# The gate's and the value's last 42 columns of a gated feed-forward as one joint block of weights

## Chip, cores and metric

The kernel runs on one core of one Trainium2 chip. The metric is the device time of one execution in microseconds (us); the time before is the median of three runs.

## What is computed

The reference runs two layers of a perceiver on x of shape 32 x 64 x 256 with a context of 32 x 1601 x 256. Each layer is a cross-attention, a self-attention or recurrent block and a feed-forward. The change concerns the gated feed-forward at the end of the recurrent block of layer 1, cut to what matters:

```
FF_INNER = int(D * 4 * 2 / 3)              # 682 with D = 256
n = _rmsnorm(x, ff_gamma)
ff = jax.nn.silu(n @ w_gate) * (n @ w_value) @ w_ff_out
x = ff * RES_SCALE + x
```

682 is 5 x 128 + 42: five full blocks of 128 columns, and a rest of 42.

## The kernel before

The 2048 rows of x are worked in 16 tiles of 128 rows. The bulk of the time is a software pipeline over the cross-attention of layer 1: 13 steps for each tile, 208 in all. Each step g issues, in this order, the column scores of g (L773, L779, then the exponential on ACT, L785), the values of g + 4 (tile vps; copied by DVE to vau, L715), the row scores of g + 5 (L731, tile r; their maxima on DVE, L738, tile mx), the weighted sum of g (L803) and the keys of g + 6 (tile kps; copied by ACT to kt, L698). The column scores and the row scores share two pairs of PSUM banks (tag sc), so the column scores of a step wait until DVE has taken the maxima of the row scores issued before.

All other layers' work is put between these parts by generators. Each `yield` is a place where a generator may stop; `yield ACT` asks to go on in the slot between values and row scores (place 0), a bare `yield` in the slot after the keys (place 1). The order on PE, DVE, ACT and POOL is the order in which the program is written and run through (a manual schedule); the DMA issues on SP are put in by the framework. The generator `tail` of one tile runs `recurrent` and then `bit_ffn`; the gated feed-forward is the last part of `recurrent`. Beside it, in the same slots, run the generators of later tiles: `query` (tp_d, copied by ACT to xT_d, then the product q) and `layer0` (tp_c, su, sv, k, q, v, tpp, o, gps).

Every small product of PE goes to one of three PSUM banks, which all these generators and vps and kps share (`mm_tile`, tag mm, three buffers). Which bank a product gets, and whose end it then waits for, is decided by the framework from the order in which earlier users give their banks back.

The feed-forward takes the normalised rows, transposed, as nT (two chunks of 128). w_fg and w_fv hold the gate's and the value's weights as six blocks of 128 columns, the last padded with zeros from column 682. The work is done in two halves of three blocks each. Per half, mm2 (L233) multiplies three blocks of the gate into one bank, then three of the value into another; an fp32 matmul is issued as two instructions, so a half has 24. Then `silu_mul` follows: tanh of half the gate on ACT (L237, tile fth), half the gate on DVE (L238, tile fm), times the value (L239), and after a yield (tanh + 1) times that (L241). The last product ffo (L946) multiplies the six blocks of fm with w_fo, whose rows past 682 are zero. In 14 of the tiles both halves fall into the pipeline; the last two tiles are worked after it, in the last 75 us, where nothing else is left to run beside them. There the seven DVE steps of the last tile's convolution (cT, L863 and L866) stand in DVE's queue behind the products of the tile before.

The weights of this part are loaded by SP in `late_weights`, between 24 and 51 us, among the loads of parts of the context (part, L95), each of which waits for ACT to have summed up the one before (L245). The first feed-forward begins at 365 us.

Of the kernel before, what the change touches and what calls it, by code (L numbers as in the profile page):

```python
# [9 lines left out]
F32 = mybir.dt.float32  # L10
BF16 = mybir.dt.bfloat16
AF = mybir.ActivationFunctionType
ALU = mybir.AluOpType
AX = mybir.AxisListType

P = 128
# [8 lines left out]
FF = 682  # L25
NF = 6
# [18 lines left out]
def perceiver_kernel(ctx: ExitStack, tc: tile.TileContext, a: dict, out: bass.AP):  # L45
    nc = tc.nc
    PSUM = bass.MemoryType.PSUM

    const = ctx.enter_context(tc.tile_pool(name="const", bufs=1))
# [19 lines left out]
    def mm_tile(shape, name, dtype=F32):  # L69
        return ps_mm.tile(shape, dtype, tag="mm", name=name)  # L70
# [115 lines left out]
    def moments(x, name):  # L186

        st = small.tile([P, 6], F32, tag="bnst", name=f"st_{name}")
        nc.vector.bn_stats(st, x)
        mv = small.tile([P, 2], F32, tag="bnmv", name=f"mv_{name}", bufs=4)  # L190
        nc.vector.bn_aggr(mv, st)
        rstd = small.tile([P, 1], F32, tag="rstd", name=f"rstd_{name}", bufs=4)
        nc.gpsimd.tensor_scalar(rstd, mv[:, 1:2], 1e-5, None, ALU.add)
        nc.gpsimd.tensor_tensor(rstd, rstd, mhalf, ALU.pow)
        return x, mv, rstd
# [34 lines left out]
    def mm2(o, lhsT, rhs):  # L230

        for c in range(2):
            nc.tensor.matmul(o, lhsT=lhsT(c), rhs=rhs(c), start=(c == 0), stop=(c == 1))  # L233

    def silu_mul(m, u, v, th):

        nc.scalar.activation(th, u, AF.Tanh, scale=0.5)  # L237
        nc.vector.tensor_scalar(m, u, 0.5, None, ALU.mult)  # L238
        nc.vector.tensor_tensor(m, m, v, ALU.mult)  # L239
        yield  # L240
        nc.vector.scalar_tensor_tensor(m, th, 1.0, m, ALU.add, ALU.mult)  # L241
# [603 lines left out]
    def recurrent(ti, x):  # L845
        def tile_(shape, tag, name):
            return work_tile(shape, tag, f"{name}_{ti}")

        m = moments(x, f"e{ti}")
# [8 lines left out]
        for c in range(2):  # L858
            nc.scalar.activation(ypad[:, c, :, 3:], t[:, c, :].rearrange("p (b s) -> p b s", b=2), AF.Copy,
                                 scale=gains[:, c, 0:1])  # L860
# [17 lines left out]
        nT = tile_([P, 2, P], "xTb", "nT")  # L878
# [14 lines left out]
        for part in range(2):  # L893
            for c in range(2):
                for h in range(2):
                    r = slice(64 * h, 64 * h + 64)
# [34 lines left out]
        nT = tile_([P, 2, P], "xTb", "nT2")  # L931
# [1 line left out]
            nc.scalar.activation(nT[:, c, :], t[:, c, :], AF.Copy, scale=gains[:, c, 2:3])  # L933
        yield ACT
        m = tile_([P, NF, P], "w4k", "fm")
        for f0 in range(0, NF, 3):
            uv = [mm_tile([P, 3, P], f"ff_{ti}_{f0}_{j}") for j in range(2)]
            for o, w in zip(uv, (w_fg, w_fv)):
                for f in range(3):
                    mm2(o[:, f, :], lambda c: w[:, c, (f0 + f) * P:(f0 + f + 1) * P], lambda c: nT[:, c, :])  # L940
            th = tile_([P, 3, P], "g2k", f"fth{f0}")
            yield from silu_mul(m[:, f0:f0 + 3, :], uv[0], uv[1], th)
            yield ACT if f0 == 0 else None
        o = mm_tile([P, D], f"ffo_{ti}")
        for f in range(NF):
# [54 lines left out]
    def tail(ti, x):  # L1000
        x = yield from recurrent(ti, x)
        yield from bit_ffn(ti, x)
# [36 lines left out]
    w_hg = const.tile([P, 2, 2 * DI], F32, name="w_hg")  # L1039
    w_go = const.tile([P, 4, 64], F32, name="w_go")  # L1040
    nc.gpsimd.memset(w_go[DI:], 0.0)
    w_fg = const.tile([P, 2, NF * P], F32, name="w_fg")
    w_fv = const.tile([P, 2, NF * P], F32, name="w_fv")
    for w in (w_fg, w_fv):
        nc.gpsimd.memset(w[:, :, FF:], 0.0)
    w_fo = const.tile([P, NF, D], F32, name="w_fo")
    nc.gpsimd.memset(w_fo[:, NF - 1, :], 0.0)

    def late_weights():
        for j in range(4):  # L1050
            nc.sync.dma_start(w_o2[32 * j:32 * j + 16],
                              a["L1_xattn_WoT"].rearrange("(g j d) o -> j d g o", j=4, d=16)[j])
            nc.sync.dma_start(bv2[32 * j:32 * j + 16], a["bv2"][j])
        nc.sync.dma_start(w_pw, a["L1_attn_pw_wT"].rearrange("(c p) o -> p c o", p=P))
        nc.sync.dma_start(w_hg, a["L1_attn_w_hg"].rearrange("(c h) d e -> (h d) c e", c=2))
        nc.sync.dma_start(w_go[:DI], a["L1_attn_w_out"].rearrange("h e o -> e h o"))
        for w, name in ((w_fg, "L1_attn_w_gate"), (w_fv, "L1_attn_w_value")):
            nc.sync.dma_start(w[:, :, :FF], a[name].rearrange("(c p) f -> p c f", p=P))
        last = (NF - 1) * P
        nc.sync.dma_start(w_fo[:, 0:NF - 1, :], a["L1_attn_w_ff_out"][0:last, :].rearrange("(f p) o -> p f o", p=P))  # L1060
        nc.sync.dma_start(w_fo[0:FF - last, NF - 1, :], a["L1_attn_w_ff_out"][last:FF, :])

# [159 lines left out]
    with tc.manual_schedule(engines={ET.PE, ET.DVE, ET.Activation, ET.Pool}):  # L1222
# [43 lines left out]
        for g in range(NU * NT):  # L1266
            pos, p = divmod(g, NU)
# [80 lines left out]
```

## Time and profile before

| | before |
|---|---|
| median of 3 runs | 2189.57 us (2186.16 to 2190.60) |
| profiled execution | 2185.15 us, span 2183.4 us |
| granted TensorE clock, mean | 0.977 |
| PE busy | 2065.7 us, 95% |
| DVE busy | 1342.4 us, 61% |
| ACT busy | 907.6 us, 42% |
| POOL busy | 325.6 us, 15% |
| matmuls ff<-nT,w_fg and ff<-nT,w_fv | 384 each, 51.6 and 49.1 us busy |
| DVE L238, L239, L241 on fm | 32 each, 17.8, 17.7 and 17.6 us busy |
| ACT L237 on fth | 32, 15.7 us busy |

A matmul's busy time overlaps with that of its neighbours, since matmuls are pipelined: the record of one 128x128 matmul is 275 ns long, while the next begins after 112 ns. What a matmul costs is therefore read from the starts. An entry "idle before <-X" names what the engine waited for. A span's time is from the first to the last instruction; the execution's own time is 1.75 us longer.

### The profile page before, as it was taken

The page shows a single profiled execution, that of the slowest core. Times are in us where ns is not written, and L with a number is a line of the kernel's source. Part 1 is how long each engine was busy: PE and PEld are TensorE (multiplying, and loading weights), DVE is VectorE, ACT ScalarE, POOL GpSimd, SP SyncE. Part 2 cuts the span into 40 slices and gives each one's busy share as a digit, 9 for nine tenths or more (in the row PEclk, how much of TensorE's full clock was granted, in tenths as well). Part 3 has the DMA queues.
Part 4 walks back from the last instruction along what each step waited for, and adds up shares of the span by engine and source line. Part 5 has one row for each costly group of instructions (what it writes and reads, how often), then busy time and mean ns, then how long its engine had stood idle before and what let it go on. Part 6 is the DMA issues. An engine that isn't in the chain of part 4 may idle for free.

```text
span 2183.4 us, 69814 instructions
## 1 busy us (share of the span) xinstructions
PE 2065.7 (95%) x31887; PEld 1510.1 (69%) x31903; DVE 1342.4 (61%) x2710; ACT 907.6 (42%) x1400; POOL 325.6 (15%) x541
## 2 busy tenths in 40 slices
PE   5799999999999999999999999999999999999984
PEld 3567677767677777777777676777777676677763
DVE  4556756666656766666666656566676665556554
ACT  3334444443535344454544435453433434334342
POOL 2111111111111111111111111111110111000011
PEclk8799999999999999999999999999999999999996
DMA  7233221211112121111211111110101101010000
GB/s 265 80 111 113 79 74 55 78 53 35 67 62 70 62 67 35 64 67 62 69 65 35 56 61 65 65 52 32 35 24 44 53 32 35 8 38 35 2 5 5
DMA packets 46176, 126.42 MB, mean 58 GB/s; under 512 B 12558, under 2 KB 28344, under 8 KB 45880
## 3 DMA queue, kind: packets, MB, share of 16 engines
q1 hardware_dynamic: 45320, 121.13, 16.2%
q8 instruction: 250, 4.10, 0.8%
q10 hardware_dynamic: 560, 0.81, 0.1%
q14 instruction: 46, 0.38, 0.1%
HBM read 119.83 MB, written 2.10 MB: 56 GB/s over the span
## 4 chain that ended last, share of the span: by engine, by line
PE 83%; DVE 11%; ACT 3%; issue 1%; DMA 1%; POOL 1%; SPq 0%; POOLq 0%; ACTq 0%; DVEq 0%
PE vps L233 16%; PE kps L233 15%; PE r L731 10%; PE o L803 9%; PE s L779 8%; PE ff L233 4%; DVE mx L738 3%; PE s L773 3%; PE ffo L946 2%; DVE vau L715 2%; PE q L233 1%; PE wo L838 1%; ACT pt L785 1%; PE hg L897 1%; PE v L319 1%
## 5 line engine op out<-in xcount | busy, mean ns | idle before, releaser
L738 DVE TENSOR_REDUCE mx<-r 128x2 f32<-128x1024 f32 x384 | 452.2, 1220 | 118.5 <-PE r L731 118.1
L785 ACT ACTIVATE pt<-s 128x1024 f32<-128x1024 f32 (+1 forms) x416 | 403.0, 1020 | 293.5 <-PE s L779 293.3
L698 ACT ACTIVATE kt<-kps,chv 128x512 f32<-128x512 f32 x192 | 131.9, 687 | 640.2 <-PE kps L233 640.2
L233 PE MATMUL vps<-w_L_xattn_WvT,ctxT 128*128 128x128 f32 x3072 | 395.1, 282 | 0.0
L233 PE MATMUL kps<-ctxT,w_L_xattn_WkT 128*128 128x512 f32 x768 | 383.2, 622 | 11.9 <-DMA ctxT<-ctxT 11.9
L233 PEld LDWEIGHTS vps<-w_L_xattn_WvT,ctxT 128*128 128x128 f32 x3072 | 359.0, 192 | 23.7 <-issue 2.8
L715 DVE COPY vau<-vps 128x512 f32<-128x512 f32 (+1 forms) x208 | 143.3, 689 | 373.0 <-PE vps L233 372.9
L803 PEld LDWEIGHTS o<-pt,vau 128*32 128x32 f32 (+1 forms) x13312 | 197.4, 110 | 150.9 <-issue 144.1
L803 PE MATMUL o<-pt,vau 128*32 128x64 f32 (+1 forms) x13312 | 232.0, 222 | 4.2 <-ACT pt L785 4.2
L731 PE MATMUL r<-kt,qbd 32*128 32x512 f32 x1536 | 228.1, 652 | 2.5 <-DVE mx L738 1.5
L233 PEld LDWEIGHTS kps<-ctxT,w_L_xattn_WkT 128*128 128x128 f32 x768 | 131.6, 191 | 123.7 <-issue 106.8
L779 PEld LDWEIGHTS s<-qbd,kt 32*128 32x128 f32 x6144 | 206.3, 187 | 3.1
L779 PE MATMUL s<-qbd,kt 32*128 32x128 f32 x6144 | 206.6, 271 | 0.0
L245 ACT ACTIVATE part<-part 128x1601 f32<-128x1601 f32 x60 | 92.6, 1543 | 15.8 <-DMA part<-ctxT 15.6
L731 PEld LDWEIGHTS r<-kt,qbd 32*128 32x128 f32 x1536 | 63.3, 185 | 40.9 <-issue 18.7
L773 PEld LDWEIGHTS <-onesb 3*128 3x128 bf16 x768 | 20.8, 91 | 91.3 <-issue 89.7
L773 PE MATMUL s<-neg,onesb 3*128 3x512 bf16 x768 | 79.0, 385 | 5.1 <-DVE mx L738 2.9
L821 DVE RECIPROCAL rs<-sums 128x128 f32<-128x128 f32 x64 | 60.7, 948 | 1.7 <-PE sums L818 1.7
L311 POOL TENSOR_TENSOR kbd<-kT,mask 128x512 f32<-128x512 f32 x32 | 32.9, 1049 | 138.0 <-ACT kT L304 138.0
L233 PE MATMUL ff<-nT,w_fg 128*128 128x128 f32 x384 | 51.6, 287 | 1.0 <-ACT nT L933 1.0
L233 PE MATMUL ff<-nT,w_fv 128*128 128x128 f32 x384 | 49.1, 278 | 0.0
L233 PEld LDWEIGHTS ff<-nT,w_fg 128*128 128x128 f32 x384 | 47.7, 200 | 1.8 <-ACT nT L933 1.6
(334 smaller groups left out, 2543.5 us busy)
## 6 DMA issues: line engine op xcount, KB each, us to landing
ctxT<-ctxT SPq DMA_DIRECT2D x32, 1601.0 KB, 7.1
part<-ctxT SPq DMA_DIRECT2D x60, 800.5 KB, 4.4
rest<-ctxT SPq DMA_DIRECT2D x32, 65.0 KB, 2.0
x<-x SPq DMA_DIRECT2D x16, 128.0 KB, 2.1
out<-x SPq DMA_DIRECT2D x16, 128.0 KB, 1.7
w<-w SPq DMA_DIRECT2D x16, 128.0 KB, 2.2
sum_L_ffn_w1T<-L_ffn_w1T SPq DMA_DIRECT2D x4, 256.0 KB, 6.6
raw_L_ffn_w1T<-L_ffn_w1T SPq DMA_DIRECT2D x4, 256.0 KB, 2.6
```

The lines of the kernel that those rows point to most:

```text
L233: nc.tensor.matmul(o, lhsT=lhsT(c), rhs=rhs(c), start=(c == 0), stop=(c == 1))
L245: nc.scalar.activation(junk, src, AF.Copy, accum_out=csum[:, c, b:b + 1])
L698: nc.scalar.activation(kt, o, AF.Identity, bias=chv[:, hf.oc, BK2:BK2 + 1])
L715: nc.vector.tensor_copy(v[:kr, :, 0:VW - 16].rearrange("p k (h d) -> p k h d", d=17)[:, :, :, 0:16], o[:kr].rearrange("p k (h d) -> p k h ...
L731: nc.tensor.matmul(o, lhsT=qbd[r, q % 2, q // 2].rearrange("p h q -> p (h q)"), rhs=w.kt[r, q, :] if h is None else halves[h].kt[k][r, :], ...
L738: nc.vector.tensor_reduce(w.mx[:, 2 * m:2 * m + 2, h % 4, k], ps[m], AX.X, ALU.max)
L773: nc.tensor.matmul(o, lhsT=onesb[r, :], rhs=halves[h].neg[r, :].unsqueeze(1).to_broadcast([3, 4, P]), start=True, stop=False)
L779: nc.tensor.matmul(ps[i // 2][:kr, i % 2, j * P:(j + 1) * P], lhsT=w.kt[r, j, :] if h is None else halves[h].kt[k][r, j * P:(j + 1) * P], ...
L785: nc.scalar.activation(pt[:kr].rearrange("p i k c -> p i (k c)"), ps[m][:kr], AF.Exp)
L803: nc.tensor.matmul(w.o[32 * c:32 * c + 32, q, m, :], lhsT=v[:kr, j, 17 * hd:17 * hd + 32], rhs=pts[m][:kr, c // 2, j, c % 2 * S:c % 2 * S ...
L821: nc.vector.reciprocal(rs, t)
L946: nc.tensor.matmul(o, lhsT=m[:, f, :], rhs=w_fo[:, f, :], start=(f == 0), stop=(f == NF - 1))
```

## The change

The second half keeps two full blocks each of gate and value. The two rests of 42 columns go into one block of weights, w_fl, the gate's at columns 0 to 41 and the value's at 64 to 105, zeros elsewhere. It is multiplied once, as the last of the half, into the third part of the gate's bank, so that the gate's rest comes out on partitions 0 to 41 and the value's rest on partitions 64 to 105 of the same columns. Tanh and halving run over all three parts as before. The multiplication by the value is split: two blocks from the value's bank, and the rest by a 64-row product that reads partitions 64 to 127 of the gate's bank and writes partitions 0 to 63 of fm. Rows 64 to 127 of the last part of fm then hold numbers that meet only zero rows of w_fo. The code of `silu_mul` is written out in place (now L946 to L953); its steps are the same in the first half.

```diff
-        for f0 in range(0, NF, 3):
+        for f0, n in ((0, 3), (3, 2)):
             uv = [mm_tile([P, 3, P], f"ff_{ti}_{f0}_{j}") for j in range(2)]
             for o, w in zip(uv, (w_fg, w_fv)):
-                for f in range(3):
+                for f in range(n):
                     mm2(o[:, f, :], lambda c: w[:, c, (f0 + f) * P:(f0 + f + 1) * P], lambda c: nT[:, c, :])
             th = tile_([P, 3, P], "g2k", f"fth{f0}")
-            yield from silu_mul(m[:, f0:f0 + 3, :], uv[0], uv[1], th)
+            if f0:
+
+                mm2(uv[0][:, 2, :], lambda c: w_fl[:, c, :], lambda c: nT[:, c, :])
+            u = uv[0][:, 0:3]
+            nc.scalar.activation(th, u, AF.Tanh, scale=0.5)
+            mf = m[:, f0:f0 + 3, :]
+            nc.vector.tensor_scalar(mf, u, 0.5, None, ALU.mult)
+            nc.vector.tensor_tensor(mf[:, 0:n], mf[:, 0:n], uv[1][:, 0:n], ALU.mult)
+            if f0:
+                nc.vector.tensor_tensor(mf[0:64, 2], mf[0:64, 2], uv[0][64:128, 2], ALU.mult)
+            yield
+            nc.vector.scalar_tensor_tensor(mf, th, 1.0, mf, ALU.add, ALU.mult)
             yield ACT if f0 == 0 else None
...
-    w_fg = const.tile([P, 2, NF * P], F32, name="w_fg")
-    w_fv = const.tile([P, 2, NF * P], F32, name="w_fv")
-    for w in (w_fg, w_fv):
-        nc.gpsimd.memset(w[:, :, FF:], 0.0)
+    w_fg = const.tile([P, 2, (NF - 1) * P], F32, name="w_fg")
+    w_fv = const.tile([P, 2, (NF - 1) * P], F32, name="w_fv")
+    w_fl = const.tile([P, 2, P], F32, name="w_fl")
+    nc.gpsimd.memset(w_fl, 0.0)
...
+        last = (NF - 1) * P
         for w, name in ((w_fg, "L1_attn_w_gate"), (w_fv, "L1_attn_w_value")):
-            nc.sync.dma_start(w[:, :, :FF], a[name].rearrange("(c p) f -> p c f", p=P))
-        last = (NF - 1) * P
+            ends = a[name].rearrange("(c p) f -> p c f", p=P)
+            nc.sync.dma_start(w, ends[:, :, :last])
+            r = 0 if w is w_fg else 64
+            nc.sync.dma_start(w_fl[:, :, r:r + FF - last], ends[:, :, last:])
```

## The prediction

> **What bounds the kernel now.** I read the page's totals and chain first, then the timeline of the stretches that the change touches, then the chain of the last 90 us.
>
> ```profile
> PE 2065.7 (95%) x31887; PEld 1510.1 (69%) x31903; DVE 1342.4 (61%) x2710; ACT 907.6 (42%) x1400; POOL 325.6 (15%) x541
> PE 83%; DVE 11%; ACT 3%; issue 1%; DMA 1%; POOL 1%; SPq 0%; POOLq 0%; ACTq 0%; DVEq 0%
> ```
>
> PE is busy 95% of the span and is 83% of the chain, so a PE instruction removed is worth its pitch, as long as PE does not then wait for something. What it could wait for is seen in the timeline of the second feed-forward half of the first x tile:
>
> ```profile
> 376.92 1.50 PE L233 MATMUL ff<-nT,w_fg 128*128 128x128 f32 x12
> 378.26 1.50 PE L233 MATMUL ff<-nT,w_fv 128*128 128x128 f32 x12
> 378.46 0.49 ACT L237 ACTIVATE fth<-ff 128x384 f32<-128x384 f32 x1 [1.32 <-PE ff L233]
> 378.98 0.56 DVE L238 TENSOR_SCALAR fm<-ff 128x384 f32<-128x384 f32 x1 [1.17 <-ACT fth L237]
> 379.60 0.38 PE L217 MATMUL tp_d<-ident,xn_d 128*128 128x128 f32 x2
> 379.80 0.56 DVE L239 TENSOR_TENSOR fm<-fm,ff 128x384 f32<-128x384 f32 x1 [0.26 <-PE ff L233]
> 379.81 0.38 PE L217 MATMUL tp_c<-ident,xn_c 128*128 128x128 f32 x2
> 380.01 0.37 ACT L223 COPY xT_d<-tp_d 128x256 f32<-128x256 f32 x1 [1.07 <-PE tp_d L217]
> ...
> 380.13 1.14 PE L731 MATMUL r<-kt,qbd 32*128 32x512 f32 x8
> 380.28 0.38 ACT L223 COPY xT_c<-tp_c 128x256 f32<-128x256 f32 x1
> ...
> 381.30 2.36 DVE L738 TENSOR_REDUCE mx<-r 128x2 f32<-128x1024 f32 x2 [0.95 <-PE r L731]
> ```
>
> PE runs through without a stop. The tanh on ACT starts as soon as the gate's blocks are done, while PE still multiplies the value's, and DVE waits for ACT because both read one PSUM bank. Below, t = 0 is the first matmul of such a half (376.92).
>
> Where PE must wait for an ACT copy, the timeline of the seventh tile shows the price: tp_a goes into the bank of tp_d and starts 0.05 us after the copy's end (1146.79 + 0.37).
>
> ```profile
> 1146.79 0.37 ACT L223 COPY xT_d<-tp_d 128x256 f32<-128x256 f32 x1 [1.07 <-PE tp_d L217]
> ...
> 1147.21 0.20 PEld L217 LDWEIGHTS tp_a<-ident,xn_a 128*128 128x128 f32 x2 [0.26 <-ACT xT_d L223]
> ```
>
> At the end of the span nothing covers anything. The chain in order of time:
>
> ```profile
> 2121.43 2.69 PE ff L233 x24
> 2124.15 0.55 DVE fm L239
> 2124.70 0.27 DVE cT L863
> ...
> 2126.64 1.58 PE ffo L946 x6
> ```
>
> Here the path runs through the product on DVE, so what DVE and ACT gain or lose counts in full.
>
> **PE: what goes.** In each of 16 tiles the second half issues 24 matmuls now (two blocks of weights, three column groups, two chunks, two instructions each). They take 379.60 - 376.92 = 2.68 us, 0.1117 each. After it, they are 8 + 8 + 4 = 20: 2.23 us, 0.45 less. Uncovered gain: 16 x 0.45 = 7.1 us. The first halves are unchanged.
>
> **ACT: what comes later.** The tanh reads the gate's bank with the joint block in it, and the joint block is multiplied last. Its last matmul starts at 19 x 0.1117 = 2.12 (the twelfth, now, at 1.23; tanh 0.31 after it, at 1.54). So the tanh runs 2.43 to 2.92 instead of 1.54 to 2.03. Queued behind it on ACT is the copy xT_d. Successive ACT instructions overlap by 0.10 (xT_c starts at 380.28, xT_d ends at 380.38), so xT_d runs 2.82 to 3.19; now it is 3.10 to 3.47, set by tp_d.
>
> **PSUM: who waits for xT_d.** The changed kernel, built and not run, shows its waits. The joint block's value half is read from the gate's bank by an extra last multiply, so that bank is given back last. The product after tp_d in PE's queue no longer goes into it (released now by L238 at 2.62, before PE gets there) but into tp_d's own bank, and waits for xT_d. That is so in nine tiles, by the operation after tp_d: tp_c (1 and 8), su (2 and 9), v (3 and 10), tpp (6), o (7), gps (12). All later PE work queues behind it. It starts at 3.19 + 0.05 = 3.24. Now tp_c, su and tpp start at 2.90, v and gps at 2.99. A stopped PE also loses 0.06 in its next step (tp_a after its wait: 0.166 to the second matmul, 0.109 unstopped). So tiles 1, 2, 6, 8, 9 lose 0.40 each, tiles 3, 10, 12 0.31 each. In tile 7 o starts at 3.24 too, and tp_a now goes into o's bank and waits for the ACT step oT: o 0.27, lag 0.29, oT 0.37, 0.05, so 4.21 instead of 3.52: 0.69. Together 2.00 + 0.93 + 0.69 = +3.62.
>
> **DVE: what it adds.** After the tanh: L948 2.95 to 3.51 (0.56), the product of two blocks instead of three 0.42 (a 128x256 product is 421 ns), to 3.97, then a new 64x128 product that reads partitions 64 to 127 and writes 0 to 63. No row has that. Bounds: from below 0.11 (a 128x4 product, L747, 191 ns, less an overlap of 0.08 as between fm L241 and xn_e in the same timeline), from above 0.63 (554 ns for three full blocks, plus the overlap lost). I take 0.31, the 128x128 product of L822 (309 ns), nearest in width. DVE is then free at 4.28 instead of 3.43.
>
> In tiles 4, 5, 11, 13 no product stands between tp_d and the row scores, and PE does arrive 0.45 earlier. But the row maxima (2.36 for the pair, at 4.17 now) start at 4.28, end at 6.64, and the next column scores wait for the second of them: 6.69 instead of the 6.56 that PE could reach (7.01 now). Gain 0.32 each: -1.28. Tile 14 has no tp_d; PE would be there at 6.34, the maxima again allow 6.69 against 6.79 now: -0.10.
>
> In tile 15 cT starts 0.08 before DVE is free: 4.20 instead of 3.35, all of it on the chain above: +0.85. In the last tile the half starts at 2157.45, its last matmul at 2159.57, the tanh 0.37 later (as there now); then tanh 0.49, L948 0.56, products 0.42 and 0.31, last fm 0.55, with 0.03 between them: its end is at 2162.38 instead of 2161.48, +0.90.
>
> **The Trainium skill** has a rule against this edit ("VectorE: DVE Perf Modes", section "Two Vector instructions with no wait between them"). A Vector instruction whose PSUM input starts in another 32-partition group than the last PSUM read is held until all earlier ones have finished, and so is the next reader from the old group. The trace shows the overlap that would be lost, 0.08; no row reads PSUM from partition 64 while another reads from 0. By the rule the sum would be some 0.4 higher; without it, as below.
>
> **Edits at nothing.** Two more DMA issues on SP (0.42 to 0.48 each) at about 45 us. SP's last issue of that group ends at 45.5, and its next waits until 50.69 for ACT to give back the part buffer; the first use of the weights is at 365. If that cover were gone, the next part load would be 0.9 late. Two memsets on POOL (265 and 231 ns at 7.4) become one; nobody waits for them.
>
> **The sum.** +3.62 - 1.28 - 0.10 + 0.85 + 0.90 = +4.0 us. With the lower bound of the product and no loss at restart it is +2.4, with the upper bound +6.2. The profiled execution is 2185.15 (span 2183.4), 4.4 under the median; I put the sum on the median: 2189.57 + 4.0 = 2193.6, by the bounds 2192.0 to 2195.8.
>
> **Rivals.**
> *Faster.* The copy is there in time and PE's saving stands: 14 x -0.45, and the end +1.75, gives -4.5, 2185.1. For it: PE is 95% busy, and xT_d itself is early enough by tp_d. Against it: the tanh sits before the copy on ACT, and 2.43 + 0.49 can't be under the 2.65 that tp_d would allow.
> *Slower.* The 64-row product is dear, since it moves data between partitions. It decides from about 0.19: from there the maxima hold the column scores in tiles 4, 5, 11, 13, 14, and each 0.1 costs 0.7 us over these and the two ends. At 1.22, the longest of DVE's large groups (L738), it gives 3.62 + 4 x 0.59 + 0.81 + 1.76 + 1.81 = +10.4, 2200.0. For it: no row of this kind. Against it: all elementwise DVE rows follow width.
> *Nothing.* Losses are absorbed by a later wait; the column scores follow the keys without a gap, so I see no such place.
>
> **Numbers.** 0.2% (4.4 us) is about what a measurement of this kernel can tell from no change. My forecast has 0.70, and 4.0 lies so near the limit that I split it 0.33 within and 0.37 above, the rule on held instructions tipping it upward. Slower rival 0.16, faster rival 0.12, nothing 0.02. So faster 0.12, same 0.35, slower 0.53. The range: the runs scatter from 2186.16 to 2190.60, 3.4 below and 1.0 above the median; from the bounds with scatter and up to the slower rival's end, 2186.5 to 2200.
>
> **What would show it.** Right: PE idle of about 0.3 us ahead of tp_c, su, v, tpp, o and gps with xT_d as releaser; the second tanh 0.9 later after its first matmul; row scores about 0.4 later in nine tiles and 0.45 earlier in five; a 64x128 row on DVE near 0.31. Wrong: no idle time of PE before these (the faster rival), or a 64x128 row of a microsecond (the slower one), or a shorter end.

## The result, and the profile after

The changed kernel takes 2193.47 us (median of 22 runs, 2184.45 to 2198.55); the kernel before, on the same chip, 2187.91 us (22 runs, 2182.33 to 2192.87). The ratio is 1.0024, 95% interval 1.0015 to 1.0033: 5.2 us slower (3.3 to 7.2). The profiled execution of the changed kernel has a span of 2184.5 us at a mean granted clock of 0.981, that of the kernel before 2183.4 us at 0.977. The two spans alone would say "+1 us". But this execution of the changed kernel is already 4.2 us ahead when the second half of the first tile begins (372.75 us against 376.92), before any changed half has run; over the first 125 us its granted clock is 0.86, that of before 0.81. So the places are read one by one below.

The page's totals and its chain, after:

```profile
PE 2056.8 (94%) x31823; PEld 1498.5 (69%) x31839; DVE 1344.0 (62%) x2726; ACT 906.5 (41%) x1400; POOL 325.3 (15%) x540
PE 82%; DVE 11%; ACT 3%; DMA 2%; issue 1%; POOL 0%; POOLq 0%; SPq 0%; ACTq 0%; DVEq 0%
```

64 matmuls fewer, 16 DVE instructions more, and PE is busy 94% instead of 95%: it has less to do and waits more. Where it waits is seen in the timeline of the second half of the first tile (columns: start, us, engine, line, operation, tiles, shapes, count, idle time before and what ended it). The half's first matmul is at 372.75. Here and in the timelines below, rows that do not bear on the point, such as weight loads, are left out.

```profile
374.54 0.61 PE L233 MATMUL ff<-nT,w_fl 128*128 128x128 f32 x4
374.99 0.38 PE L217 MATMUL tp_d<-ident,xn_d 128*128 128x128 f32 x2
375.19 0.49 ACT L946 ACTIVATE fth<-ff 128x384 f32<-128x384 f32 x1 [2.21 <-PE ff L233]
375.57 0.37 ACT L223 COPY xT_d<-tp_d 128x256 f32<-128x256 f32 x1
375.71 0.56 DVE L948 TENSOR_SCALAR fm<-ff 128x384 f32<-128x384 f32 x1 [2.06 <-ACT fth L946]
376.00 0.44 PE L217 MATMUL tp_c<-ident,xn_c 128*128 128x128 f32 x2 [0.62 <-ACT xT_d L223]
376.30 0.42 DVE L949 TENSOR_TENSOR fm<-fm,ff 128x256 f32<-128x256 f32 x1
376.36 1.14 PE L731 MATMUL r<-kt,qbd 32*128 32x512 f32 x8
376.74 0.29 DVE L951 TENSOR_TENSOR fm<-fm,ff 64x128 f32<-64x128 f32 x1
```

tp_d starts 2.24 after the first matmul, 0.45 earlier than before. tp_c starts at 3.25 instead of 2.89, and its bracket names xT_d. ACT has no idle time between tanh and xT_d: the copy is not waiting for PE, it is queued behind the tanh, and the tanh waited for the joint block, the last thing that PE multiplies.

In the seventh tile, o waits for xT_d and tp_a then for oT:

```profile
1146.89 0.37 ACT L223 COPY xT_d<-tp_d 128x256 f32<-128x256 f32 x1
1147.31 0.43 PE L385 MATMUL o<-pT,vbd 128*32 128x64 f32 x16 [0.62 <-ACT xT_d L223]
1147.81 0.37 ACT L388 ACTIVATE oT<-o,chv 128x128 f32<-128x128 f32 x1 [0.55 <-PE o L385]
1148.23 0.44 PE L217 MATMUL tp_a<-ident,xn_a 128*128 128x128 f32 x2 [0.49 <-ACT oT L388]
```

And at the end of the span, in the chain in order of time, PE's part is shorter (2.25 for 2.69), but four steps of ACT and DVE now stand between it and cT where one did:

```profile
2121.45 2.25 PE ff L233 x20
2123.72 0.50 ACT fth L946
2124.24 0.57 DVE fm L948
2124.83 0.42 DVE fm L949
2125.27 0.29 DVE fm L951
2125.56 0.27 DVE cT L863
2125.85 0.36 DVE cT L866
```

To price places without the scatter of whole runs, I took for each of the 14 tiles in the pipeline the time from the start of the values' product (vps) ahead of the second half to the start of the second column scores after it, and subtracted the same time in the trace of before. In windows without a change these differences are at most 0.01 us.

| tiles | predicted | after | e4 | e5 | e7 | e8 |
|---|---|---|---|---|---|---|
| 1, 8 | +0.40 | +0.40 | +0.24 | -0.30 | -0.45 | +0.40 |
| 2, 9 | +0.40 | +0.44 | +0.28 | +0.62 | -0.27 | +0.44 |
| 3, 10 | +0.31 | +0.25 | +0.09 | -0.45 | -0.45 | +0.25 |
| 12 | +0.31 | +0.25 | +0.09 | +0.01 | -0.45 | +0.25 |
| 6 | +0.40 | +0.46 | +0.30 | -0.45 | -0.45 | +0.46 |
| 7 | +0.69 | +0.63 | -0.09 | -0.06 | -0.10 | +0.08 |
| 4, 5, 11, 13 | -0.32 | -0.30 | -0.45 | -0.08 | -0.45 | -0.45 |
| 14 | -0.10 | -0.20 | -0.45 | -0.20 | -0.45 | -0.45 |
| sum of 14 | +2.24 | +2.13 | -0.73 | -1.30 | -5.56 | +0.74 |

The columns e4 to e8 are experiments told below.

### The profile page after: what moved, and what is told of

Same layout as the page of the kernel before. It is cut to its first block, busy times and chain, and to the rows that moved or that the text cites. A ratio compares the mean times of both kernels' runs of the same rounds, so it can differ in the third digit from the quotient of the medians.

```text
span 2184.5 us, 69689 instructions
## 1 busy us (share of the span) xinstructions
PE 2056.8 (94%) x31823; PEld 1498.5 (69%) x31839; DVE 1344.0 (62%) x2726; ACT 906.5 (41%) x1400; POOL 325.3 (15%) x540
## 4 chain that ended last, share of the span: by engine, by line
PE 82%; DVE 11%; ACT 3%; DMA 2%; issue 1%; POOL 0%; POOLq 0%; SPq 0%; ACTq 0%; DVEq 0%
PE vps L233 16%; PE kps L233 16%; PE r L731 10%; PE o L803 9%; PE s L779 8%; PE ff L233 4%; PE s L773 3%; DVE mx L738 3%; PE ffo L957 2%; DVE vau L715 2%; PE wo L838 1%; ACT pt L785 1%; PE q L233 1%; DMA part<-ctxT 1%; PE hg L897 1%
## 5 line engine op out<-in xcount | busy, mean ns | idle before, releaser
L779 PEld LDWEIGHTS s<-qbd,kt 32*128 32x128 f32 x6144 | 206.4, 187 | 3.1
L779 PE MATMUL s<-qbd,kt 32*128 32x128 f32 x6144 | 207.3, 271 | 0.0
L773 PE MATMUL s<-neg,onesb 3*128 3x512 bf16 x768 | 79.9, 385 | 5.1 <-DVE mx L738 2.9
L773 PEld LDWEIGHTS <-onesb 3*128 3x128 bf16 x768 | 21.2, 91 | 91.8 <-issue 90.0
L948 DVE TENSOR_SCALAR fm<-ff 128x384 f32<-128x384 f32 x32 | 17.8, 557 | 58.0 <-ACT fth L946 58.0
L957 PE MATMUL ffo<-w_fo,fm 128*128 128x256 f32 x192 | 44.6, 380 | 3.8 <-DVE fm L953 3.8
L957 PEld LDWEIGHTS ffo<-w_fo,fm 128*128 128x128 f32 x192 | 36.1, 190 | 15.4 <-issue 6.7
```

The lines of the kernel that those rows point to most:

```text
L773: nc.tensor.matmul(o, lhsT=onesb[r, :], rhs=halves[h].neg[r, :].unsqueeze(1).to_broadcast([3, 4, P]), start=True, stop=False)
L779: nc.tensor.matmul(ps[i // 2][:kr, i % 2, j * P:(j + 1) * P], lhsT=w.kt[r, j, :] if h is None else halves[h].kt[k][r, j * P:(j + 1) * P], ...
L957: nc.tensor.matmul(o, lhsT=m[:, f, :], rhs=w_fo[:, f, :], start=(f == 0), stop=(f == NF - 1))
```

## The experiments

Each was timed against the kernel before on the same chip: 21 to 33 runs of before, 7 to 11 of the experiment. Rival A: the product across partitions is what costs. Rival B: the loss belongs to no place. Others are named where they come up.

**e1, e2, e3: the change by places.** Both layouts of the weights are loaded, and a set of tiles decides:

```diff
-        for f0, n in ((0, 3), (3, 2)):
+        for f0 in (0, 3):
+            joint = f0 and ti in (4, 5, 11, 13, 14)   # e1; the nine: e2; (15, 0): e3
+            n = 2 if joint else 3
...
-            if f0:
+            if joint:
```

(ti 0 is tile 16.)

> The joint block only in tiles 4, 5, 11, 13, 14 (no product of PE stands between tp_d and the row scores there, or no tp_d at all); all other tiles as before. My theory (PE's saving is real, and only a product that goes into tp_d's bank and waits for xT_d turns it into a loss): -0.32 in each of four tiles and -0.10 in tile 14, together -1.4 us, ratio 0.9994, with PE 0.30 to 0.45 earlier after each of the five and no wait. Rival A (every 64-row product across partitions costs the same, wherever it stands: 5.2 us over 16 tiles, 0.33 each): +1.6 us, ratio 1.0007. Rival B (the loss is one of the whole program, such as its loads, not of these places): +5 us, ratio 1.0024.

Measured: ratio 0.9988 (0.9979 to 0.9997), -2.6 us (-4.6 to -0.7). Rivals A and B fall: five products across partitions stand in this kernel, and it is faster than before. The table's window gives -0.30 in each of the four tiles and -0.20 in tile 14, together -1.39.

> The joint block only in tiles 1, 2, 3, 6, 7, 8, 9, 10, 12, where a product follows tp_d. My theory: +3.6 us by the steps of the prediction (0.40 in five tiles, 0.31 in three, 0.69 in tile 7), ratio 1.0017, and PE idle about 0.3 us with xT_d as what ended it in each of the nine. Rival A (0.33 for each product across partitions): +2.9 us, ratio 1.0013, without such idle times. Rival B: +5 us, ratio 1.0024, whichever tiles are changed.

Measured: 1.0026 (1.0012 to 1.0040), +5.7 us (2.6 to 8.8). By windows +3.53, the same nine numbers as in the changed kernel. The time alone does not separate the theories; the idle times of PE, which rival A has no reason for, do: 0.62 to 0.72 before each of the nine products, ended by xT_d.

> The joint block only in tiles 15 and 16, which are worked after the pipeline. My theory: +0.85 and +0.90, together +1.75 us, ratio 1.0008, all of it in the last 75 us. Rival A (0.33 for each product): +0.65 us, ratio 1.0003. Rival B: +5 us, ratio 1.0024. If my theory holds, the three runs e1, e2 and e3 add up to what the whole change does.

Measured: 0.9999 (0.9990 to 1.0008), -0.2 us (-2.2 to +1.8). My +1.75 is at the very edge; rival B falls, rival A (+0.65) does not by the time alone. The profile shows tile 15 at +0.85 and the last tile at only +0.37: its own steps are longer by 0.90 as expected, but its first matmuls came quicker (see the hardware section). The three times, -2.6, +5.7 and -0.2, add up to +2.9, where the whole change takes 5.2 (3.3 to 7.2): with 2 to 3 us of interval on each this neither confirms nor refutes that they add up. The windows do add up, place by place.

**e4: the joint block second.** It is multiplied between the gate's and the value's blocks.

```diff
             for o, w in zip(uv, (w_fg, w_fv)):
                 for f in range(n):
                     mm2(o[:, f, :], ...)
+                if f0 and w is w_fg:
+                    mm2(uv[0][:, 2, :], lambda c: w_fl[:, c, :], lambda c: nT[:, c, :])
...
-            if f0:
-
-                mm2(uv[0][:, 2, :], lambda c: w_fl[:, c, :], lambda c: nT[:, c, :])
```

> All tiles changed, but the joint block is multiplied between the gate's and the value's blocks, so that the gate's bank is full after the twelfth matmul, as before. My theory: tanh again at 1.54 to 2.03, xT_d then set by tp_d alone, 2.65 to 3.02 (now 2.82 to 3.19), the product after tp_d still goes into tp_d's bank and starts at 3.07 (now 3.24, before 2.90 or 2.99): +0.23 in five tiles, +0.14 in three, about -0.1 in tile 7; DVE is free at about 3.37, so tiles 4, 5, 11, 13, 14 gain the full 0.45 each, and the two ends about 0.06 each. Together -0.9 us, ratio 0.9996: some 6 us under the change as made. Rival A (the product across partitions): the order of PE's products does not matter, +5 us, ratio 1.0024. Rival B: the same, +5 us.

Measured: 1.0005 (0.9995 to 1.0015), +1.1 us (-1.1 to +3.3). Rivals A and B, which gave +5, lie outside. The timeline of the first tile (first matmul at 378.88):

```profile
380.42 0.49 ACT L945 ACTIVATE fth<-ff 128x384 f32<-128x384 f32 x1 [1.32 <-PE ff L233]
381.11 0.38 PE L217 MATMUL tp_d<-ident,xn_d 128*128 128x128 f32 x2
381.53 0.37 ACT L223 COPY xT_d<-tp_d 128x256 f32<-128x256 f32 x1 [0.62 <-PE tp_d L217]
381.95 0.44 PE L217 MATMUL tp_c<-ident,xn_c 128*128 128x128 f32 x2 [0.46 <-ACT xT_d L223]
```

The releaser of xT_d is now tp_d, with 0.62 of idle ACT before it, and tp_c starts at 3.07 as expected. So the late tanh was 0.17 of each wait. The rest is left because PE arrives earlier and still waits for the bank that ACT empties. Whether the gate's bank, which the 64-row product still reads last here, would have been free sooner without that product was not run. Tiles 4, 5, 11, 13, 14 keep the full 0.45.

**e5, e6, e7: the query's step ahead of the half.** In the slot where a second half is issued, tp_d goes first; e5 is the changed kernel, e6 the kernel before, e7 has the edit of e4 as well.

```diff
-    ACT = "ACT"
+    ACT, HALF, QUERY = "ACT", "HALF", "QUERY"
...
         xn = normalised(work_tile([P, D], "xnq", f"xn_d{ti}"), m)
-        yield ACT
+        yield QUERY
...
-            yield ACT if f0 == 0 else None
+            yield HALF if f0 == 0 else None
...
-                if (self.kind == ACT) != (place == 0):
+                if (self.kind in (ACT, HALF)) != (place == 0):
...
-            for s in [s for s in plan if s.t0 <= t]:
+            steps = [s for s in plan if s.t0 <= t]
+            if place == 0 and any(s.kind == HALF for s in steps):
+                steps.sort(key=lambda s: s.kind != QUERY)
+            for s in steps:
```

> The changed kernel, its joint block last as it is, with one edit: in the slot in which a second half is issued, the query's step (tp_d, xT_d) goes ahead of it. xT_d is then done before the tanh, and the product after the half goes into the bank of vps, free at 0.89. My theory: the nine waits for xT_d are gone; what is left is DVE, free at 4.5 instead of 3.4: about -0.1 in tiles 4, 5, 11, 13, -0.2 to -0.45 in 1, 3, 6, 8, 10, 12, 14, +0.5 in tiles 2 and 9 (sv waits for the value's bank), nothing in 7, +1.3 to +1.8 in the two ends. Together about 0, ratio 1.0000, some 4 to 5 us under the change as made. Rival A (each product across partitions costs 0.33): +5 us, ratio 1.0024, since all sixteen stay. Rival C (the order of the slot is what is tuned, any move costs): more than +5 us.

Measured: 1.0020 (1.0011 to 1.0028), +4.4 us (2.4 to 6.1). A miss: I expected about 0, and by the time alone rival A (+5) would fit. In the pipeline the profile does what was expected, -1.30 by windows, with a product across partitions in each of the 14 tiles, which rival A would put at +4.6; the nine waits for xT_d are gone. But its last stretch, from the first matmul of tile 15's first half to the end, takes 72.9 us against 67.9, 4.9 more and not 1.3 to 1.8.

> The kernel before with the same move of the query's step ahead of the second half, and nothing else: the control to e5 and e7. My theory: no wait of PE on xT_d lay on the path before, so it gives nothing but 0.2 in tile 7 (tp_a): -0.2 us, ratio 0.9999. Rival A: 0. Rival C (moving the step is itself a gain or a loss): 2 us or more either way, ratio 0.999 or 1.001.

Measured: 0.9996 (0.9987 to 1.0005), -0.9 us (-2.8 to +1.1). By windows only tile 7 moves, -0.17. Moving the step is worth next to nothing while PE has its 24 matmuls ahead of the next product. A gain of 2 us (rival C) still lies inside the interval, a loss of 2 us does not; no window shows either.

> Both edits: the joint block between the gate's and the value's blocks (tanh at 1.54 from the half's first matmul) and the query's step ahead of the half. My theory: nothing waits, so PE's 0.45 is kept: -0.45 in ten tiles, -0.31 in tiles 2 and 9 (sv waits for the value's bank), -0.1 in tile 7, -0.2 in tile 14, -0.15 in the two ends; together -5.6 us, ratio 0.9974, faster than both kernels. Rival A (product across partitions): +5 us less what the order gives, not under the kernel before. Rival D (PE's saving is given back by the clock, which is granted lower the busier PE is): no change, ratio 1.000.

Measured: 0.9979 (0.9970 to 0.9988), -4.6 us (-6.6 to -2.6). This version beats both kernels, with the same weights, the same 20 matmuls and the same product across partitions as the changed one. The first tile (first matmul of the half at 377.29):

```profile
377.07 0.38 PE L217 MATMUL tp_d<-ident,xn_d 128*128 128x128 f32 x2
377.49 0.37 ACT L223 COPY xT_d<-tp_d 128x256 f32<-128x256 f32 x1 [0.19 <-PE tp_d L217]
378.83 0.49 ACT L945 ACTIVATE fth<-ff 128x384 f32<-128x384 f32 x1 [0.97 <-PE ff L233]
379.52 0.38 PE L217 MATMUL tp_c<-ident,xn_c 128*128 128x128 f32 x2
379.83 1.14 PE L731 MATMUL r<-kt,qbd 32*128 32x512 f32 x8
```

xT_d is done at 377.86, the tanh has ACT to itself, and tp_c and r carry no bracket: PE runs through. Tile 14 and ten others keep the full 0.45. Rivals A and D (the clock takes the saving back) fall.

**e8: without the 64-row product.**

```diff
-            if f0:
-                nc.vector.tensor_tensor(mf[0:64, 2], mf[0:64, 2], uv[0][64:128, 2], ALU.mult)
```

> The changed kernel without the 64-row product: the rest's gate is not multiplied by the rest's value, all else is left. The product after tp_d still goes into tp_d's bank. My theory: the nine waits stay as they are (in tile 7 tp_a no longer waits for oT, +0.1 instead of +0.64): +3.0; DVE is free 0.31 earlier, so tiles 4, 5, 11, 13 gain the full 0.45 (-1.8) and tile 14 0.2; the ends +0.5 and +0.6. Together +2 us, ratio 1.0009. Rival A (the product across partitions is the loss): under the kernel before, by PE's saving, -4 us or more, ratio 0.998.

Measured: 1.0014 (1.0003 to 1.0025), +3.1 us (0.7 to 5.5). Still slower than before, so rival A falls once more. Timeline of the first tile (first matmul at 377.52):

```profile
380.34 0.37 ACT L223 COPY xT_d<-tp_d 128x256 f32<-128x256 f32 x1
380.48 0.56 DVE L948 TENSOR_SCALAR fm<-ff 128x384 f32<-128x384 f32 x1 [2.06 <-ACT fth L946]
380.76 0.44 PE L217 MATMUL tp_c<-ident,xn_c 128*128 128x128 f32 x2 [0.62 <-ACT xT_d L223]
```

tp_c waits for xT_d exactly as with the product, although the gate's bank is now given back by L948, at 381.04. So with the joint block last, the wait does not come from the extra product.

**e9: e5 with the two ends as before.** (`joint = f0 and 1 <= ti <= 14`, as in e1.)

> As e5 (joint block last, query's step ahead of the half), but tiles 15 and 16 as in the kernel before. e5 came out 3 us above its expectation; its profile has the fourteen tiles of the pipeline at -1.3 us, as expected, and 4.9 us more in the last 75 us, with 23 and 27 slow matmuls (0.213 us instead of 0.112) after PE's pauses there, where the kernel before has 17 and 17. My theory: the pipeline's part is -1.3 us, ratio 0.9994, and the rest of e5 lay in the two ends. Rival E (the joint block last costs time in the pipeline that the profile of one run does not show): +1 us or more, ratio 1.0005 or more.

Measured: 1.0009 (0.9999 to 1.0018), +2.0 us (-0.2 to +3.9). By windows -1.27 in the pipeline, as in e5. The time is 2.4 us lower than e5's, which fits a part of e5's miss in the ends, though the two intervals overlap; -1.3 is outside the interval, and rival E is not refuted (more on this at the end).

**e10: the product five times at the ends.** Otherwise as e3.

```diff
-                nc.vector.tensor_tensor(mf[0:64, 2], mf[0:64, 2], uv[0][64:128, 2], ALU.mult)
+                for _ in range(5):
+                    nc.vector.tensor_tensor(mf[0:64, 2], mf[0:64, 2], uv[0][64:128, 2], ALU.mult)
```

> As e3 (joint block only in tiles 15 and 16), with the 64-row product issued five times there (so the rest is multiplied by its value five times). My theory: at the ends DVE is on the path in full, and each further product costs 0.31 us, its 0.29 and the gap to the next: 8 x 0.31 = +2.5 over e3, +4.2 us in all by the steps of the prediction, ratio 1.0019, a little less if the slow matmuls at the start of the last tile come out fewer. Rival A (such a product is dear): each 0.6 or more, +7 us, ratio 1.003. Rival F (the ends have slack): as e3, 0 to +1 us, ratio 1.000.

Measured: 1.0026 (1.0017 to 1.0035), +5.7 us (3.7 to 7.7). The ends have no slack (rival F falls). The time allows both my +4.2 and the +7 of rival A; the timeline of the last tile gives the price, against 0.6 and more of rival A:

```profile
2164.73 1.58 DVE L954 TENSOR_TENSOR fm<-fm,ff 64x128 f32<-64x128 f32 x5
2166.35 0.56 DVE L956 SCALAR_TENSOR_TENSOR fm<-fth,fm 128x384 f32<-128x384 f32 x1
```

Five take 1.58: 0.29 each, 0.324 from one to the next.

## Why the prediction was right, step by step

**PE's saving** is real: tp_d starts 0.45 earlier in all thirteen tiles that have one, and e7 keeps 0.45 in eleven of fourteen tiles.

**The late tanh and the nine waits** came as predicted, with the operations and the releaser named: +3.53 against +3.62. The size that I gave for the sign, PE idle about 0.3, was wrong: it reads 0.62 to 0.72 from the end of tp_d's record, and my own steps gave 3.24 - (2.23 + 0.38) = 0.63. Tiles 3, 10, 12 lose 0.25 and not 0.31 (the 0.06 at the restart does not arise there). Tile 6 loses 0.46 for 0.40: tpp starts at 3.33.

**The bank** was right in effect and wrong in its reason. I put it on the extra product that gives the gate's bank back last. e8 has no such product and the same wait; with the joint block last, L948 ends at 3.52 after the first matmul, later than xT_d at 3.19, so tp_d's bank is the one that is free first in any case. What I did not see is the bound behind it: e4 shows that even with the tanh as early as before, PE comes back to a bank that ACT is still emptying, and 0.45 of saving turns into +0.24 in tiles 1 and 8. The way out was to move the consumer (e7), not the joint block alone.

**The 64-row product** was taken at 0.31 and takes 0.29. The row behind the lower bound, L747, has a median of 165 ns; one of 1.8 us lifts its mean to the 191 that I used. What the Trainium skill ("VectorE: DVE Perf Modes", "Two Vector instructions with no wait between them") says of held instructions is seen here. In tile 4, where the maxima follow:

```profile
769.18 0.42 DVE L949 TENSOR_TENSOR fm<-fm,ff 128x256 f32<-128x256 f32 x1
769.62 0.29 DVE L951 TENSOR_TENSOR fm<-fm,ff 64x128 f32<-64x128 f32 x1
769.94 2.36 DVE L738 TENSOR_REDUCE mx<-r 128x2 f32<-128x1024 f32 x2
```

L951, reading PSUM from partition 64, starts 0.02 after L949's end; mx, from partition 0 again, 0.03 after L951's (769.91). In tile 7, mT, which reads no PSUM, starts at 1148.28, 0.08 before L951's end (1148.36). The control is e8, which has no such product; there mx starts 0.08 before L949's end:

```profile
773.47 0.42 DVE L949 TENSOR_TENSOR fm<-fm,ff 128x256 f32<-128x256 f32 x1
773.81 2.35 DVE L738 TENSOR_REDUCE mx<-r 128x2 f32<-128x1024 f32 x2
```

A held reader so loses about 0.1 of overlap. From the half's first matmul, mx starts at 4.30 with the product and at 3.89 without: the product is worth 0.41 there, of which 0.29 is its own. In the sum the holds are small, since I had put the maxima behind the product's end without an overlap: tiles 4, 5, 11, 13 gain 0.30 for 0.32. Tile 14 gains 0.20 for 0.10; I had put its column scores at 6.69, and two of the four matmuls of L773 start at 6.34 without a wait, the other two at 6.71.

**The edits at nothing** delayed nothing that the trace shows: SP's issues of that group end at 46.3, and its next part load is issued at 50.32 (before, 50.69).

**The ends.** Tile 15: +0.848 in e3, predicted +0.85; in the profile of the changed kernel cT starts 0.84 later, but the stretch from the half to the last tile's first matmul is only 0.58 longer. The last tile: from the first matmul of the half to the last fm 4.92 instead of 4.03, +0.90 as predicted; but in the profile of the changed kernel the half itself began 0.32 earlier after the tile's first matmul, so the two ends together show +1.0 there.

**The sum.** Predicted +4.0; by windows and ends the profile gives 2.13 + 1.0 = +3.1; measured 5.2 (3.3 to 7.2). The difference of about 2 us lies between the windows, where nothing was changed: there the trace of the changed kernel loses a further 2.05. Two dips of the clock in each trace cancel (see the hardware section). What is left are places where PE stands still in the middle of the column scores (L779) and the profile shows nothing that it waits for ("issue"). In the trace of before there is one:

```profile
436.05 0.44 PE L779 MATMUL s<-qbd,ktr 32*65 32x128 f32 x5 [0.61 <-issue]
```

In that of the changed kernel there are two:

```profile
432.95 0.43 PE L779 MATMUL s<-qbd,ktr 32*65 32x128 f32 x2 [1.25 <-issue]
686.84 0.32 PE L779 MATMUL s<-qbd,ktr 32*65 32x128 f32 x1 [1.22 <-issue]
```

They put the work behind them off by 0.65 and 1.41. From the first window to the end the traces so give 2.13 + 2.05 + 1.02 = +5.2. This is one trace of each kernel, and it does not show that the change makes such stops longer: e6, with the weights and matmuls of before, has two of 1.54 and 0.90, its trace gives about +2 in this way without its dips of the clock, and it was measured at -0.9; e3 and e10 have one stop of about 0.7. So my steps account for about +3.1, and the cause of the rest is open. That the forecast of 2193.6 met the measured 2193.47 so closely is luck: its base was 1.66 above the median of the 22 runs of before, and its change 1.2 below the measured one. My rivals fell: the copy is not in time (faster), the product is cheap (slower), and the interval excludes no change (nothing).

## What to carry to other kernels

Work taken from the busiest engine pays only if what that engine does next is ready earlier too: follow the next instructions to the buffer they write and to whoever empties it, and move that consumer along with the saving. When a block is folded into a tile that an early reader needs whole, multiply it before that reader's cut, not last. Where whole runs scatter by more than the effect, sum differences over short windows of the trace, each anchored to the same instruction in both kernels, and then read what is left between the windows too.

## What the hardware showed beside this

**The granted clock goes with the scatter.** The 22 runs of the changed kernel have mean clocks of 0.973 to 0.981 and spans of 2196.8 to 2182.7 us. A straight line through all runs here, each kernel about its own mean, gives about 1.4 us for each 0.001 (correlation about -0.8). Inside the pipeline the clock is full but for dips of 3.4 us at half (0.50 from 1709.5 to 1712.9 in the trace of before). Most of them come at five places, near 725, 1206, 1711, 1895 and 1981 us; each trace has some of them and not others. Two stretches, first after, then before (columns: window, length, PE, PEld, DVE, ACT, POOL busy, clock, DMA share, GB/s):

```profile
1708.00:1716.00 8.00, 6.62 (x160) 4.80 (x159) 5.87 (x14) 3.27 (x6) 1.64 (x4) 1.00 0.57 207
1977.00:1984.00 7.00, 6.71 (x144) 4.29 (x144) 2.92 (x5) 1.32 (x4) 2.38 (x4) 0.76 0.62 233
```

```profile
1708.00:1716.00 8.00, 7.82 (x156) 5.79 (x157) 4.65 (x12) 1.71 (x5) 3.28 (x7) 0.79 0.51 200
1977.00:1984.00 7.00, 6.10 (x153) 4.17 (x152) 3.75 (x7) 2.73 (x5) 2.28 (x4) 1.00 0.66 237
```

Each dip is a step of about 1.6 us between the two traces, and none of these places is touched by the change.

**After a pause PE starts slow, for a varying time.** In the first half of tiles 15 and 16, matmuls follow each other at 0.213 us first, at a granted clock of 0.50 (before, 2152.9 to 2156.4), and at 0.112 later. Before, 17 were slow in each; over the twelve kernels it was 13 to 27, so one such start took from 0.4 us less to 1 us more. e5's profile has 23 and 27, the 27 reaching into the second half. e1, e2, e6 and e9 have the ends of before: 15 to 17 were slow in the first three, but 23 and 22 in e9. The Trainium skill ("TensorE: Matmul & The Clock Gate", "Part 1: The HAM clock gate") says that the clock is released by a free-running window of activity, so that the number of slow matmuls differs between runs of the same kernel; the counts differ here too. It puts the slow time at about 3.4 us; here it was 2.8 to 5.8 us.

**What stays open.** e5 and e9 took about 4 and 3 us more than their windows and predicted ends give, the changed kernel about 1 to 2. The mean clocks of e5 and e9 are lower than that of before in the same session (0.9754 and 0.9757 against 0.9767 and 0.9764); by the line above that is worth 1 to 2 us. So a third to a half of it goes with the clock. Their profiles also have the stops of PE told above, three each (0.77, 0.77 and 0.83 in e5; 0.49, 0.80 and 0.84 in e9), against the one of 0.61 before. In e9's profile the stops put work off by 2.2 more than before, and its unchanged ends take 1.3 longer, mostly by slow starts; with the -1.27 of the windows that is +2.2, where +2.0 was measured. Whether a kernel with the joint block last is granted a lower clock or stops more often for a reason, or these were draws of the same scatter (e10, which touches only the ends, had 0.9750), no run here tells.
